# A two-layer graph attention and a transformer block on one core: order of adjacency loads, clips and the first comparison in the opening

## The chip, the cores and the metric

One Trainium2 chip, one of its cores. The metric is the device time of one execution in microseconds (us), the median of several executions. Engines are named as in the profile: PE is the matrix engine (PEld its weight loads), DVE the vector engine, ACT the scalar engine, POOL the general-purpose engine, SP the engine whose queue issues the transfers (SPq in the trace).

## The reference

x has 4096 rows of 256 numbers, and adj is a 4096 x 4096 matrix of 0 and 1 (int32). There are 8 heads of 32 columns.

```python
def gat_layer(x, adj, W, a):
    Wh  = einsum('nd,hdo->hno', x, W)
    src = einsum('hno,ho->hn', Wh, a[:, :O])
    dst = einsum('hno,ho->hn', Wh, a[:, O:])
    e = leaky_relu(src[:, :, None] + dst[:, None, :], 0.2)
    e = where(adj > 0, e, -9e15)
    return einsum('hnm,hmo->hno', softmax(e), Wh)      # heads side by side

h = elu(gat_layer(x, adj, W1, a1)) + x
x = elu(gat_layer(h, adj, W2, a2)) + h
# then one transformer block: layer norm, q k v, masked attention with the same adj,
# projection, residual, layer norm, gelu feed-forward, residual
```

Only the beginning of the first graph layer is touched here.

## The kernel before

**How a graph layer is computed.** The exponential of a leaky ReLU of a sum has one of two forms, according to the sign of src + dst. The kernel therefore needs, for each head and pair of nodes, only a bit that says which form holds (a comparison of a row of terms with one number per partition), masked with the adjacency. The values, scaled for each form, stand on the other side of a matmul. The 4096 result rows are cut into four blocks (nb) of 1024, the 8 heads into four pairs (p), and the 4096 neighbours into eight groups (g) of four tiles of 128. One triple (nb, p, g) of a layer is one group i of the main loop; there are 256 in the two layers.

For group i:

- `compare(i)` makes t8: for each of four tiles k (mt = 4 g + k) and each head j of the pair, a 128 x 1024 comparison of the row s_b with `L.negd`. On ACT it is a Sign (L1122 in the profile), on DVE a tensor_scalar (L1124). Head 0 is mostly DVE's, head 1 ACT's. A fifth step, `mask` (L1137, on DVE), joins t8 with the adjacency mask.
- PE multiplies 128 x 128 pieces of t8 and of the mask with the values vst (L1463).

Other work is put between the matmuls of a group by fractions of the group's length: the comparison of group i + 2, the preparation of values for later tiles, and the adjacency for later groups.

**Adjacency.** One unit (nb, c, k) is 256 rows by 512 columns of adj, 512 KB. `mask_load` brings it into g_adj (three buffers), `mask_clip` (L867, DVE) turns it into 8-bit numbers in adj_8 (five buffers), `turn_out` transposes it on PE (L892) into one of two turn banks, and `turn_in` copies it from there to the mask on ACT (L898). After every second unit SP writes a piece of the mask to memory (mask_d, L901). Outside the opening each clip issues one more load.

**Preparation** of four tiles (`preparation`): the rows of x are transposed (L991) and copied on ACT to g_ft (L1000); the values are multiplied (L1005); ACT and DVE take four kinds of terms from them (L1018 to L1020 on ACT; L1023, L1036 and L1045 on DVE); `split` puts them into vst as a high half (L1051 on ACT) and a low half (L1054 on POOL). At last the terms of head rows go through g_sr (L1065) to memory (s_d, L1068). From there `s_fetch` reads them back as s_b, one row copied to all 128 partitions, for each head of the pair (L1095).

**The opening** is `begin`. In it the order on PE, ACT, DVE and SP is the order of the program (`manual_schedule`); after it this holds for PE, ACT and DVE, while the order on SP is found by the scheduler. SP's small loads for later stages (e_x, e_terms, and the layer norm's n_g and n_be) are put between by the scheduler too. `begin` handles the adjacency for groups 0 and 1 of block 0: units 0 to 7 (the first three in g_adj, four in buffers of the mask, one in a buffer of t8). `turns[0]` holds units 8 to 11, which group 0 transposes. f_0, v_0, part_0, row_0 are the steps of the preparation of the first four tiles, f_1 to row_1 those of the next four; each is a pair of an out step (PE) and an in step (ACT, DVE).

The lines that decide who makes which comparison:

```python
if (j == 1 or mt in more) and not (i == 0 and k == 0):
    nc.scalar.activation(to.bitcast(I8), s, AF.Sign, bias=negd, scale=-1.0)
else:
    nc.vector.tensor_scalar(to, s, negd, -1.0, op0=ALU.is_ge, op1=ALU.mult, saturate=False)
```

So in group 0 DVE makes head 0 of all four tiles and head 1 of the first, ACT the other three.

Of the kernel before, what the change touches and what calls it, by code (L numbers as in the profile page):

```python
# [751 lines left out]
def graph_attention(  # L752
# [38 lines left out]
    G = 4  # L791
# [61 lines left out]
    def mask_load(nb, c, i, r=None):  # L853

        if r is None:
            r = rows_p.tile([P, 2, G * P], I32, name="g_adj", bufs=3)
        at = STARTS[0][nb] * P + i * 2 * P
        nc.sync.dma_start(
            r,
            adj[at : at + 2 * P, c * G * P : (c + 1) * G * P].rearrange("(k r) m -> k r m", r=2),  # L860
        )
        loaded[nb, c, i] = r

    def mask_clip(nb, c, i, load=True):

        v = rows_p.tile([P, G * P, 2], F8, name="adj_8", bufs=5)
        nc.vector.tensor_scalar(  # L867
            v.rearrange("p m r -> p r m"),
            loaded.pop((nb, c, i)),
            1.0,  # L870
            -(2.0**-30),
            op0=ALU.min,
            op1=ALU.max,
            saturate=False,
        )
        clipped[nb, c, i] = v.rearrange("p m r -> p (m r)").bitcast(F16)
        if load:
            load_ahead(1)
# [26 lines left out]
    def mask_turn(nb, c, i):  # L905
        turn_out(nb, c, i)
        turn_in(nb, c, i)
# [17 lines left out]
    def weights_load(l):  # L925

        w, a = weights[l]
        L = Layer()
        L.a_sb = ep.tile([P, H, 2, O], F32, name="e_terms")
        nc.sync.dma_start(  # L930
            L.a_sb.rearrange("p h s o -> p (h s o)"), spread(a, [[0, P], [1, H * 2 * O]])
        )
        L.w_ext = keep.tile([P, DC, D + 2 * H], F32, name="g_w_ext")
        for c in range(DC):
            nc.sync.dma_start(
                L.w_ext[:, c, 0:D].rearrange("p (h o) -> p h o", o=O),
                w[:, c * P : (c + 1) * P, :].rearrange("h p o -> p h o"),
            )
        L.terms = keep.tile([P, 2, NT, H], F32, name=f"g_terms{l}")
        L.negd = L.terms[:, 1]  # L940
        L.r = keep.tile([P, NT, H], F32, name=f"g_r{l}")
        L.tops = keep.tile([P, NT], F32, name=f"g_tops{l}")
        L.ft = {}
        layers.append(L)

    def weights_steps(l):

        L = layers[l]
        values_ = L.w_ext[:, :, 0:D]
        terms = L.w_ext[:, :, D:].rearrange("p c (k h) -> p c k h", k=2)  # L950
        held = {}

        def step_times(k):
            wa = some.tile([P, H, 2, V1], F32, name="g_prod").rearrange("p h i v -> p (h i v)")
            held[k] = wa[:, : DC * D].rearrange("p (c h o) -> p c h o", c=DC, o=O)
            nc.vector.tensor_tensor(
                held[k],
                values_.rearrange("p c (h o) -> p c h o", o=O),
                L.a_sb[:, :, k, :].unsqueeze(1).to_broadcast([P, DC, H, O]),
                op=ALU.mult,  # L960
            )

        def step_sums(k):
            nc.vector.tensor_reduce(terms[:, :, k, :], held.pop(k), AX.X, ALU.add)

        def step_ends():
            nc.vector.tensor_scalar(terms[:, :, 1, :], terms[:, :, 1, :], -1.0, None, op0=ALU.mult)
            nc.vector.tensor_scalar(values_, values_, UP, None, op0=ALU.mult)

        steps = []  # L970
        for k in range(2):
            steps += [lambda k=k: step_times(k), lambda k=k: step_sums(k)]
        return steps + [step_ends]

    def rows_ahead(l, q, width=D):
        if q < NG:
            r = coming_rows[l, q] = rows_p.tile([P, G, D], F32, name="g_rows")
            rows[l].load(r[:, :, :width], G * q, slice(0, width))
# [119 lines left out]
    def apart(i):  # L1098
        l, nb, p, g = groups[i]
        free = (l > 0 and nb + p > 0) or (nb + 1 == len(TILES[l]) and p + 1 < H // 2)  # L1100
        return g == 6 and free and i < len(groups) - NG

    def compare(i):

        l, nb, p, g = groups[i]
        L, s_b = layers[l], s_of[l, nb, p]
        t8 = s8[i] = t_p.tile([P, 2, NW, G, HB], F8, name="t8")
        more = (7, 11, 15, 23, 27, 31)
        if l > 0 or (nb + 1 == len(TILES[l]) and p + 1 < H // 2):
            more = (3, 7, 11, 15, 19, 23, 27)  # L1110
        if apart(i):
            u8[i] = [rows_p.tile([P, NW, G, HB], F8, name="g_adj", bufs=3) for j in range(2)]

        def step(k):
            mt = g * G + k
            for j in range(2):
                to = t8[:, j, :, k, :]
                s = s_b[:, j, :].rearrange("p (w n) -> p w n", n=HB)
                negd = L.negd[:, mt, 2 * p + j : 2 * p + j + 1]

                if (j == 1 or mt in more) and not (i == 0 and k == 0):
                    nc.scalar.activation(to.bitcast(I8), s, AF.Sign, bias=negd, scale=-1.0)  # L1122
                else:
                    nc.vector.tensor_scalar(  # L1124
                        to, s, negd, -1.0, op0=ALU.is_ge, op1=ALU.mult, saturate=False
                    )

        def mask():
            both = t8.rearrange("p j w g n -> p j (w g n)").bitcast(I32)
            m32 = masks[l, nb][g].rearrange("p w g n -> p (w g n)").bitcast(I32)  # L1130
            for j, u in enumerate(u8.get(i, ())):
                nc.vector.scalar_tensor_tensor(
                    u.rearrange("p w g n -> p (w g n)").bitcast(I32),
                    t8[:, j].rearrange("p w g n -> p (w g n)").bitcast(I32),
                    -1, m32, op0=ALU.bitwise_xor, op1=ALU.bitwise_and,
                )
            nc.vector.scalar_tensor_tensor(  # L1137
                both, m32.unsqueeze(1).to_broadcast(list(both.shape)), SIGNS, both,
                op0=ALU.bitwise_or, op1=ALU.bitwise_and,
            )  # L1140

        return [lambda k=k: step(k) for k in range(G)] + [mask]

    def pair_end(l, nb, p, ev):
# [100 lines left out]
    turns = {}  # L1245
# [3 lines left out]
    for nb in range(1, len(TILES[0])):  # L1249
        units = [(nb, c, k) for c in range(NG) for k in range(2 * NW)]  # L1250
# [21 lines left out]
    def load_ahead(n):  # L1272
        for _ in range(min(n, len(coming))):
            mask_load(*coming.pop(0))
# [13 lines left out]
    def begin():  # L1288

        weights_load(0)  # L1290
        rows_ahead(0, 0)
        rows_ahead(0, 1)

        units = own[: 2 * 2 * NW]
        del coming[: len(units)]
        for k, u in enumerate(units):
            place = None
            if 3 <= k < 7:
                place = mask_p.tile([P, 2, G * P], I32, name="mask")
            elif k == 7:  # L1300
                place = t_p.tile([P, 2, G * P], I32, name="t8")
            mask_load(*u, place)

        def clip(k):
            mask_clip(*units[k], load=False)

        def turn(k):
            mask_turn(*units[k])

        def both(use):  # L1310
            use[0]()
            use[1]()

        (f_0, v_0, part_0, row_0), (f_1, v_1, part_1, row_1) = (
            preparation(0, q, spare_bank, True) for q in range(2)
        )
        for use in f_0 + f_1:
            both(use)
        for step in weights_steps(0):
            step()  # L1320
        for use in v_0[:2]:
            both(use)
        for k in range(2):
            clip(k)
            both(v_0[2 + k])
        both(row_0)
        for k in range(4):
            both(v_1[k])
            part_0[k]()
            if k < 2:  # L1330
                clip(2 + k)
            if k > 1:
                part_1[k - 2]()
        both(row_1)
        s_of[0, 0, 0] = s_fetch(0, 0, 0)
        rows_ahead(0, 2)
        for k in range(4):
            turn(k)
            if k < 2:
                part_1[2 + k]()  # L1340
            clip(4 + k)
        load_ahead(3)
        ahead = turns[0]
        for step in compare(0):
            step()
        for k in range(4, len(units)):
            turn(k)
            mask_clip(*ahead[k - 4])
        for step in compare(1):
            step()  # L1350

# [5 lines left out]
    for i, (l, nb, p, g) in enumerate(groups):  # L1357
# [40 lines left out]
        if i + 2 < len(groups):  # L1398
            steps = compare(i + 2)
# [32 lines left out]
        for n in range(tiles):  # L1432
            w, at = n // PER, slice(n % PER * P, (n % PER + 1) * P)
            for m in range(G):
                s_of_m = [t8[:, j, w, m, at] for j in range(2)]
                heads = vst[g][:, m, 2 * p : 2 * p + 2]
# [949 lines left out]
```

## Time and profile before

| | us |
|---|---|
| median of 3 runs | 3108.01 |
| lowest and highest | 3107.69, 3109.81 |
| the profiled execution, its own time | 3108.51 |
| its span in the profile | 3106.7 |
| first matmul of group 0 (L1463) starts | 39.95 |

The span is what the profile shows from the first to the last instruction; the rest of an execution's time lies around it. Times in the trace are counted from the start of the span. A row of the trace's order of time gives the start, the time until the end of the last instruction in it, engine, line, operation, the tiles written and read, the number of instructions, and in brackets how long the engine had been idle before and what ended that. A stretch of the table of windows gives busy times of the engines within it.

### The profile page before, as it was taken

How to read it: one execution, taken by the hardware profiler on the slowest of the kernel's cores; microseconds unless marked ns; L12 is line 12 of the kernel's file. 1: busy time of each engine (PE TensorE's matmuls, PEld its weight loads, DVE VectorE, ACT ScalarE, POOL GpSimd, SP SyncE). 2: the span in 40 equal slices, each digit the busy share in tenths (PEclk: the TensorE clock that was granted, in tenths of full speed). 3: DMA queues.
4: the chain of work that ended last, by engine and by line, in shares of the span. 5: the costliest groups of instructions: out<-in, count | busy, mean ns of one | idle time of the engine just before them, and what ended most of it. 6: DMA issues, size and time to landing. Idle time of an engine off the chain costs nothing.

```text
span 3106.7 us, 139282 instructions
## 1 busy us (share of the span) xinstructions
PE 3057.2 (98%) x64008; PEld 2716.1 (87%) x64008; DVE 2744.0 (88%) x3105; ACT 2702.0 (87%) x3369; POOL 1263.6 (41%) x567
## 2 busy tenths in 40 slices
PE   6999999999999999999999999999999999999999
PEld 5899999999889999999986888888888888887766
DVE  7999999999989999999986999999999999997221
ACT  6899999999999999999975999999999999997232
POOL 3300000000230000000001999999999999997110
PEclk8999999999999999999999999999999999999999
DMA  8666555431221212112126101010101010013210
GB/s 259 218 200 203 169 173 173 148 91 39 88 67 30 91 57 89 38 57 64 47 87 193 32 24 35 21 42 28 31 25 34 22 38 28 28 34 102 75 34 22
DMA packets 214036, 251.15 MB, mean 81 GB/s; under 512 B 89216, under 2 KB 134528, under 8 KB 213440
## 3 DMA queue, kind: packets, MB, share of 16 engines
q1 hardware_dynamic: 213440, 242.15, 25.2%
q8 instruction: 502, 8.22, 1.1%
q14 instruction: 94, 0.77, 0.1%
HBM read 199.63 MB, written 42.47 MB: 78 GB/s over the span
## 4 chain that ended last, share of the span: by engine, by line
PE 51%; ACT 1%; DVE 1%; issue 0%; DVEq 0%; ACTq 0%
PE u_ps L1897 15%; PE u_av L1929 14%; PE u_dn L1929 8%; PE misc L2262 4%; PE misc L2238 4%; PE bank L1463 3%; PE misc L1834 2%; ACT t L1122 1%; PE misc L1853 1%; PE misc L2197 1%; PE misc L1556 0%; DVE t L1137 0%; PE u_ps L2093 0%; DVE t L1124 0%; DVE u_e L1908 0%
## 5 line engine op out<-in xcount | busy, mean ns | idle before, releaser
L1463 PE MATMUL bank<-vst,t 128*128 128x132 f16 x16384 | 1456.6, 220 | 3.6 <-DVE t L1137 3.0
L1463 PE MATMUL bank<-vst,mask 128*128 128x132 f16 (+1 forms) x10516 | 1372.9, 206 | 0.0
L2145 POOL TENSOR_TENSOR u_both<-u_e 128x1024 f32<-128x1024 f32 x446 | 1044.2, 2387 | 768.8 <-DMA u_k<-half_d 768.5
L1122 ACT ACTIVATE t<-s_b,g_terms 128x1024 int8<-128x1024 f32 x1234 | 1318.6, 1149 | 20.1 <-PE bank L1463 15.2
L1463 PEld LDWEIGHTS <-t 128*128 128x128 fp8e4 x16384 | 1186.0, 96 | 15.8 <-DVE t L1137 5.4
L1908 DVE SCALAR_TENSOR_TENSOR u_e<-u_mask,u_ps 128x1024 f32<-128x1024 uint8 x993 | 1128.3, 1214 | 23.6 <-ACT u_ps L1907 23.2
L1907 ACT ACTIVATE u_ps<-u_ps 128x1024 f32<-128x1024 f32 x993 | 995.6, 1009 | 84.1 <-PE u_ps L1897 29.8
L1463 PEld LDWEIGHTS <-mask 128*128 128x128 fp8e4 x10516 | 921.5, 98 | 0.0
L1137 DVE SCALAR_TENSOR_TENSOR t<-mask,t 128x2048 int32<-128x2048 int32 x256 | 588.1, 2297 | 74.6 <-ACT t L1122 66.2
L1897 PE MATMUL u_ps<-u_q,u_k 128*32 128x512 f16 x8192 | 632.7, 380 | 0.7 <-DVE u_e L1908 0.7
L1929 PE MATMUL u_av<-u_e,u_v 128*32 128x128 f32 x16384 | 602.7, 273 | 0.0
L1124 DVE TENSOR_SCALAR t<-s_b,g_terms 128x1024 fp8e4<-128x1024 f32 x814 | 590.8, 759 | 1.9 <-DMA s_b<-s_d 1.9
L1929 PEld LDWEIGHTS u_av<-u_e,u_v 128*32 128x32 f32 x16384 | 483.6, 110 | 119.6 <-ACT u_ps L1907 0.3
L1054 POOL TENSOR_TENSOR vst<-g_adj,vst 128x528 f16<-128x528 f32 x16 | 19.9, 1241 | 725.7 <-ACT g_big L1018 681.6
L1929 PE MATMUL u_dn<-u_both,u_ones 128*32 128x128 f32 x7136 | 278.4, 273 | 0.0
L1929 PEld LDWEIGHTS u_dn<-u_both,u_ones 128*32 128x32 f32 x7136 | 212.4, 110 | 51.4 <-issue 0.8
L1897 PEld LDWEIGHTS <-u_k 128*32 128x32 f16 x8192 | 231.2, 96 | 18.0 <-issue 3.0
L2245 ACT ACTIVATE u_hid<-misc,n_b 128x512 f32<-128x512 f32 x64 | 43.9, 687 | 140.6 <-PE misc L2238 140.6
L2262 PE MATMUL misc<-u_k,u_hid 128*128 128x256 f32 x512 | 111.9, 380 | 0.0
L2262 PEld LDWEIGHTS misc<-u_k,u_hid 128*128 128x128 f32 x512 | 96.9, 190 | 13.2 <-issue 0.5
L2238 PE MATMUL misc<-ln_cols,u_k 128*128 128x512 f32 x224 | 97.3, 593 | 0.0
L867 DVE TENSOR_SCALAR adj<-g_adj 128x1024 fp8e4<-128x1024 int32 x123 | 89.0, 725 | 3.0 <-DMA g_adj<-in_adj_dram 3.0
(195 smaller groups left out, 1927.7 us busy)
## 6 DMA issues: line engine op xcount, KB each, us to landing
g_adj<-in_adj_dram SPq DMA_DIRECT2D x123, 512.0 KB
s_b<-s_d SPq DMA_DIRECT2D x64, 512.0 KB
mask<-mask SPq DMA_DIRECT2D x128, 256.0 KB
u_mask<-mask SPq DMA_DIRECT2D x64, 256.0 KB
mask<-stage SPq DMA_DIRECT2D x48, 256.0 KB
half_d<-u_halves SPq DMA_DIRECT2D x32, 256.0 KB
u_q<-half_d SPq DMA_DIRECT2D x32, 256.0 KB
rows<-e_x SPq DMA_DIRECT2D x31, 256.0 KB
```

The source lines that it names most:

```text
L867: nc.vector.tensor_scalar(v.rearrange("p m r -> p r m"), loaded.pop((nb, c, i)), 1.0, -(2.0**-30), op0=ALU.min, op1=ALU.max, saturate=False,)
L1122: nc.scalar.activation(to.bitcast(I8), s, AF.Sign, bias=negd, scale=-1.0)
L1124: nc.vector.tensor_scalar(to, s, negd, -1.0, op0=ALU.is_ge, op1=ALU.mult, saturate=False)
L1137: nc.vector.scalar_tensor_tensor(both, m32.unsqueeze(1).to_broadcast(list(both.shape)), SIGNS, both, op0=ALU.bitwise_or, op1=ALU.bitwise_and,)
L1463: nc.tensor.matmul(to, left, right, start=k not in opened, stop=last)
L1897: nc.tensor.matmul(ps[r * O : (r + 1) * O, j, :], k_st[c][:, 2 * u + j, at : at + O], q_st[:, h, :], start=True, stop=True,)
L1907: nc.scalar.activation(ps, ps, AF.Exp, scale=SCALE)
L1908: nc.vector.scalar_tensor_tensor(e, mask, 0.0, ps, op0=ALU.not_equal, op1=ALU.mult)
L1929: nc.tensor.matmul(to[j * O : (j + 1) * O, at], lefts[j], es[j // 2][:, j % 2, at], start=first and part == 0, stop=last and part == PARTS ...
L2145: nc.gpsimd.tensor_tensor(both, es_of[i - 1][u], es_of[i][u], op=ALU.add)
L2238: nc.tensor.matmul(ph, w1_sb[:, k, f * P : (f + 1) * P], hn[:, k, :], start=(k == 0), stop=(k == DC - 1),)
L2262: nc.tensor.matmul(po[:, :D], hid[:, f, at : at + P], w2_sb[:, f, :], start=(f == 0), stop=(f == FC - 1),)
```

## The change

In the first comparison (`compare(0)`) the steps are ordered by head: the four tiles of head 0 first, then the four of head 1. Of head 1 two tiles instead of one are made on DVE, the other two on ACT.

In `begin`, the clips of units 4 and 5 and the turn of unit 0 are put between the value steps of the second preparation, and the loads of units 8 to 10 are issued after clip 4 instead of after clip 7. The turns of units 1 to 4 and the clips of units 6 to 9 stand ahead of the comparison of group 0; the turns of units 5 to 7 and the clips of units 10 and 11 stand within and behind it. No operation is added or removed but for the one comparison that goes from ACT to DVE. After `begin` the program is the same.

```diff
-        def step(k):
+        def step(k, heads=(0, 1)):
             mt = g * G + k
-            for j in range(2):
+            for j in heads:
...
-                if (j == 1 or mt in more) and not (i == 0 and k == 0):
+                if (j == 1 or mt in more) and not (i == 0 and k < 2):
...
+        if i == 0:
+            return [lambda k=k, j=j: step(k, (j,)) for j in range(2) for k in range(G)] + [mask]
         return [lambda k=k: step(k) for k in range(G)] + [mask]
...
         both(row_0)
+        ahead = turns[0]
         for k in range(4):
+            if k == 2:
+                clip(4)
+                load_ahead(3)
+            if k == 3:
+                turn(0)
+                clip(5)
             both(v_1[k])
             part_0[k]()
...
         s_of[0, 0, 0] = s_fetch(0, 0, 0)
         rows_ahead(0, 2)
-        for k in range(4):
-            turn(k)
-            if k < 2:
-                part_1[2 + k]()
-            clip(4 + k)
-        load_ahead(3)
-        ahead = turns[0]
-        for step in compare(0):
+        for k in range(2):
+            turn(1 + k)
+            part_1[2 + k]()
+            clip(6 + k)
+        for k in range(2):
+            turn(3 + k)
+            mask_clip(*ahead[k])
+        steps = compare(0)
+        for step in steps[:G]:
             step()
-        for k in range(4, len(units)):
-            turn(k)
-            mask_clip(*ahead[k - 4])
+        turn(5)
+        for step in steps[G : 2 * G]:
+            step()
+        mask_clip(*ahead[2])
+        steps[-1]()
+        turn(6)
+        mask_clip(*ahead[3])
+        turn(7)
         for step in compare(1):
             step()
```

## The prediction

> **What bounds the kernel now.** I read the busy shares first, then a table of stretches, then the order of time on each engine in the opening.
>
> ```profile
> PE 3057.2 (98%) x64008; PEld 2716.1 (87%) x64008; DVE 2744.0 (88%) x3105; ACT 2702.0 (87%) x3369; POOL 1263.6 (41%) x567
> ```
>
> TensorE is busy 98% of the span, so the 2% that it waits is all that a change of order can win. Where that lies is in the table (columns: stretch, its length, PE, PEld, DVE, ACT, POOL busy, granted clock, DMA share, GB/s):
>
> ```profile
> 20.00:30.00 10.00, 3.25 (x27) 2.29 (x26) 7.41 (x17) 6.36 (x20) 9.22 (x8) 0.71 0.48 118
> 30.00:40.00 10.00, 1.84 (x16) 1.29 (x14) 7.60 (x9) 5.56 (x9) 0.64 (x1) 0.50 0.95 305
> 40.00:50.00 10.00, 7.91 (x69) 6.99 (x69) 6.87 (x9) 8.31 (x17) 0.00 (x0) 0.76 0.78 242
> 50.00:60.00 10.00, 8.38 (x89) 7.22 (x90) 9.83 (x21) 6.69 (x16) 4.68 (x3) 0.83 0.93 309
> 80.00:90.00 10.00, 8.87 (x118) 7.63 (x116) 10.00 (x19) 8.04 (x20) 6.15 (x4) 1.00 0.89 260
> 140.00:160.00 20.00, 20.00 (x383) 20.00 (x381) 19.65 (x23) 20.00 (x26) 0.00 (x0) 1.00 0.67 224
> ```
>
> Three stages: up to 50 us all engines have gaps; from 50 to about 120 us DVE is full and sets the pace; from 140 us TensorE is full. In the second stage the mask steps (L1137) start at 60.69, 74.57, 88.50, 102.36 and 116.23, one group of 13.87 us after the other. So a microsecond saved before 50 us on the chain that feeds DVE is handed on to the end, if nothing in between needs a fixed time. That chain, in order of time on DVE, ACT and PE:
>
> ```profile
> 31.11 0.69 DVE L867 TENSOR_SCALAR adj<-t 128x1024 fp8e4<-128x1024 int32 x1
> 34.34 2.74 DVE L1124 TENSOR_SCALAR t<-s_b,g_terms 128x1024 fp8e4<-128x1024 f32 x4 [1.89 <-DMA s_b<-s_d]
> 37.60 2.29 DVE L1137 SCALAR_TENSOR_TENSOR t<-mask,t 128x2048 int32<-128x2048 int32 x1 [0.52 <-ACT t L1122]
> 44.80 0.70 DVE L867 TENSOR_SCALAR adj<-g_adj 128x1024 fp8e4<-128x1024 int32 x1 [3.02 <-DMA g_adj<-in_adj_dram]
> 47.59 2.29 DVE L1137 SCALAR_TENSOR_TENSOR t<-mask,t 128x2048 int32<-128x2048 int32 x1
> 50.40 0.42 DVE L1023 TENSOR_REDUCE g_tops<-turn 128x1 f32<-128x256 f32 x1
> ```
>
> ```profile
> 34.34 3.23 ACT L1122 ACTIVATE t<-s_b,g_terms 128x1024 int8<-128x1024 f32 x3 [4.25 <-DMA s_b<-s_d]
> 39.69 5.29 ACT L1122 ACTIVATE t<-s_b,g_terms 128x1024 int8<-128x1024 f32 x5
> ```
>
> ```profile
> 39.95 0.40 PE L1463 MATMUL bank<-vst,t 128*128 128x132 f16 x2 [0.78 <-DVE t L1137]
> 45.51 0.38 PE L892 MATMUL turn<-g_ident_h,adj 128*128 128x128 f16 x4 [1.34 <-DVE adj L867]
> 51.47 0.53 PE L892 MATMUL turn<-g_ident_h,adj 128*128 128x128 f16 x4 [2.22 <-DVE ev_broad L1036]
> ```
>
> Head 1's row of s_b lands at 34.34 (head 0's by 31.71). Then three signs on ACT, the mask of group 0, four late turns on ACT, five signs of group 1, and the mask of group 1 at 47.59. DVE also sits 3.0 us for an adjacency load issued only at about 40.5, since g_adj has three buffers. The wait of PE at 45.51 is put down to DVE, but DVE's clip there feeds a later turn; the turn bank it needs is freed by ACT's g_ft copy (44.89), queued behind the five signs.
>
> **Adjacency loads further ahead.** Three loads (units 8 to 10) move from SP's 30.53 to behind the first four s_d writes (end 19.23). They wait for clips 0 to 2 (the last ends at 21.36), so they run in 19.3 to 25 us, where the stretches show DMA at 0.48; they pass the second four s_d writes (ready at 23.25). Their bytes leave the crowded 28 to 39 us, and the 3.0 us wait goes: the next load (unit 11) needs only clip 8, so it is issued at about 31 to 33 instead of 40.5. What is late next is ACT, below.
>
> **SP's other order.** As built, four n_ loads (24.86 to 26.79 on SP, some 1,000 tiny packets in 26 to 28 us) leave the place ahead of s_b for later, and e_x and e_terms, before at 19.27 and 19.77 (2.1 us of full DMA in 20 to 23 us), take that place. The second g_sr copy waits for one turn copy more (0.58), so s_d is written 0.6 later. s_b was issued at 26.96 without a wait; now at 26.4 to 27.4, its first bytes at 28.5 against 28.0. I take its second row at 34.85, half a microsecond late. Ends: 33.3, if its slow tail (123 to 184 GB/s in 30 to 32 us) runs at the 300 of the s_b load in 57 to 59 us; 36.5, if everything moved ahead of it stays in its way. The second s_b pair moves from 54.7 and 65.6 to about 48 and 51, the n_ loads into 60 us and later.
>
> **Clips 4 and 5 under POOL.** They move to 22.9 and 26.2 us, where DVE idled 1.81 and 0.78 us. POOL runs its subtractions there without a break:
>
> ```profile
> 22.32 1.67 POOL L1054 TENSOR_TENSOR vst<-ev_broad,vst 128x528 f16<-128x528 f32 x1
> 23.94 1.15 POOL L1054 TENSOR_TENSOR vst<-g_prod,vst 128x528 f16<-128x528 f32 x1
> ```
>
> The first had a clip (22.30, 0.69) beside it and took 0.52 longer; a clip that met POOL at 29.6 took 1.64 instead of 0.69. By the Trainium skill, SBUF — State Buffer, section "Who interferes with whom", DVE in a two-port mode and POOL exclude each other for a whole instruction. The row agrees, and the rule speaks against the change: the gap is not free. Worked out: POOL 22.9 to 24.0, clip 4 to 24.6, POOL to 25.7 (was 25.1), product, POOL to 26.8 and 27.95, clip 5 to 28.6, last products done at 29.75 (was 28.44). Four clips, as before, take 3.36: DVE is free at 33.1, against 31.7 without the rule.
>
> **The comparison by heads.** DVE does head 0 at once (four, 2.74): to 35.85. Two tiles of head 1 follow (0.67 each, one more on DVE than before): 37.2. Clip 10 (0.65): 37.85. Mask 2.29: 40.15, against 39.89. The first step alone gains nothing: TensorE starts 0.25 late.
>
> **ACT.** Turns 0, 4 and 5 move forward into gaps of PE (3.25 of 10 us busy in 20 to 30) and of ACT; the third write of mask_d follows turn 5 on SP, now behind the loads of units 11 and 12, and nobody waits for it in the opening. ACT signs two tiles (2.15) from 34.85, copies two turns instead of four (1.05; the others ran while it sat idle for 4.25), and signs five (5.29): 43.35, against 44.98. Mask 1 then ends at 45.65 (was 49.88), since neither the load nor clips 8 to 10 stand between, and the next clip at 46.25. g_ft's first half is copied by 43.85.
>
> **TensorE to DVE.** From its start to the turn at 45.51 PE worked 4.25 (44.2 less 39.95). So it comes there at 44.45, with the bank free. From that turn to the terms on ACT it took 2.3 (45.51 to 47.81): DVE's first g_tops can start at 46.8, later than DVE's own 46.25. Before: 50.40. **Gain 3.6 us.** The 2.22 wait at 51.47 goes with it (PE arrives when the bank is free). From here the order on DVE, ACT, PE and POOL is that of before.
>
> By the bounds: without the lock 4.1; with s_b at 33.3 and no lock 5.1; with s_b at 36.5, 2.5. I keep the lock and 34.85, each nearest to a row. The profiled run took 3108.51 for a span of 3106.7, 0.50 above the median 3108.01; the span becomes 3103.1 and the median 3104.4.
>
> **The rivals.**
> A larger gain. For: PE ran group 0's start at half clock (0.32 per matmul, later 0.22), so if it is warm its 4.25 shrink by some 1.4. Against: it idles 30.7 to 38.1 as before. With s_b at 33.3 and no lock, 5.1 + 1.4 = 6.5: 3101.5.
> Nothing arrives. DVE, earlier by 3.6, meets adjacency loads that are not, and waits as it did at 44.80. For: DMA share 0.93 in 50 to 60, with s_b moved into it. Against: no such wait after 44.80 in the trace, and a load has 9.5 us from its issue to its clip. 3108.0.
> Slower. The broadcast pair and the tiny n_ loads, now in the DVE-bound stage, make loads land late in every group. It decides from where a load takes over 9.5 us; 2 us late in each of five groups is +10 - 3.6: 3114.4. Against: an s_b row takes 3 us of the queue and only two are moved.
> That s_b itself is late shows a loss only from 34.34 + 4.4 = 38.7 us on, beyond my bound.
>
> **How the numbers follow.** 0.2% is 6.2 us, about what a measurement of this kernel can tell from no change; so my forecast, a gain, counts as no change. Forecast (2.5 to 5.1 gained): 0.68. Larger gain: 0.14, nearly all past 6.2. Nothing arrives: 0.10. Slower: 0.08. Range 3101.0 to 3108.2: forecast, nothing, and the near part of the larger gain. Faster 0.14, same 0.78, slower 0.08.
>
> **What would show it.** Right: g_adj loads on SP in 19 to 25 us; clip 4 stretched to about 1.7 us; s_b's wait on ACT ending near 34.9; five signs directly after two turns, ending near 43.4; no 3.0 wait of DVE for g_adj; mask 1 at 43.4; g_tops near 46.8; mask steps still 13.87 apart. Wrong: s_b past 36.5 or before 33.3, DVE waiting for g_adj after 50 us, or mask steps with another distance.

## The result, and the profile after

| | before | after |
|---|---|---|
| median, us (19 runs each, side by side) | 3108.26 | 3103.35 |
| lowest and highest | 3107.49, 3110.15 | 3102.19, 3105.72 |
| ratio, 95% interval | | 0.9983, 0.9977 to 0.9989 |
| profiled execution: its own time / its span | 3108.51 / 3106.7 | 3105.72 / 3103.8 |

The changed kernel is 4.9 us (0.17%) faster. The forecast was 3104.4 with a gain of 3.6: a real gain, since the interval is 1.9 us to either side, but inside the 0.2% (6.2 us) that the forecast took for about the least that can be told from no change. The profiled execution of after is the longest of its 19, so its trace shows only 2.9 us of the 4.9. A second profile of the same kernel ("after_again" below) took 3102.72, nearer to the median. The two are read together, because the step in which they differ turned out to be the one that decides.

The busy shares of after, and its stretches with the columns as before:

```profile
PE 3054.6 (98%) x64008; PEld 2714.1 (87%) x64008; DVE 2743.6 (88%) x3106; ACT 2701.2 (87%) x3368; POOL 1265.6 (41%) x567
```

```profile
20.00:30.00 10.00, 2.59 (x24) 1.82 (x23) 9.29 (x19) 6.05 (x16) 9.22 (x7) 0.80 0.70 228
30.00:40.00 10.00, 1.32 (x11) 0.82 (x8) 7.50 (x10) 3.85 (x7) 0.65 (x1) 0.50 0.97 301
40.00:50.00 10.00, 8.51 (x76) 7.78 (x77) 8.47 (x11) 8.53 (x17) 0.00 (x0) 0.68 0.83 263
50.00:60.00 10.00, 8.72 (x115) 7.46 (x113) 9.48 (x18) 8.67 (x20) 5.46 (x4) 1.00 0.91 305
80.00:90.00 10.00, 9.02 (x111) 7.80 (x109) 10.00 (x14) 7.74 (x23) 5.46 (x4) 1.00 0.83 250
140.00:160.00 20.00, 20.00 (x380) 20.00 (x378) 19.64 (x23) 20.00 (x24) 0.00 (x0) 1.00 0.68 203
```

The DMA share in 20 to 30 us rose from 0.48 to 0.70: the three adjacency loads are there. In 30 to 40 us the memory traffic is as dense as before, and ACT is busy less. From 80 us on the rows are much the same. The order of time on DVE, ACT, PE and SP in after (one comparison more on DVE; L1478 is before's L1463):

```profile
33.63 2.74 DVE L1124 TENSOR_SCALAR t<-s_b,g_terms 128x1024 fp8e4<-128x1024 f32 x4 [1.83 <-DMA s_b<-s_d]
36.84 1.42 DVE L1124 TENSOR_SCALAR t<-s_b,g_terms 128x1024 fp8e4<-128x1024 f32 x2 [0.47 <-DMA s_b<-s_d]
39.06 2.29 DVE L1137 SCALAR_TENSOR_TENSOR t<-mask,t 128x2048 int32<-128x2048 int32 x1 [0.20 <-ACT t L1122]
45.22 2.29 DVE L1137 SCALAR_TENSOR_TENSOR t<-mask,t 128x2048 int32<-128x2048 int32 x1 [1.27 <-ACT t L1122]
48.38 0.42 DVE L1023 TENSOR_REDUCE g_tops<-turn 128x1 f32<-128x256 f32 x1 [0.26 <-ACT g_terms L1020]
```

```profile
36.84 2.19 ACT L1122 ACTIVATE t<-s_b,g_terms 128x1024 int8<-128x1024 f32 x2 [5.96 <-DMA s_b<-s_d]
39.89 5.30 ACT L1122 ACTIVATE t<-s_b,g_terms 128x1024 int8<-128x1024 f32 x5
```

```profile
41.41 0.40 PE L1478 MATMUL bank<-vst,t 128*128 128x132 f16 x2 [9.89 <-DVE t L1137]
```

```profile
18.39 3.67 SPq L858 DMA_DIRECT2D g_adj<-in_adj_dram  x3
23.52 1.28 SPq L1068 DMA_DIRECT2D s_d<-g_sr  x4
25.54 0.77 SPq L930 DMA_DIRECT2D e_terms<-in_L_gnn_a_dram  x1
28.13 0.81 SPq L1095 DMA_DIRECT2D s_b<-s_d  x2
```

The 3.02 us wait of DVE for an adjacency load is gone, and no adjacency load is waited for after it. What holds DVE now is s_b (1.83 and 0.47) and then ACT's five signs (1.27). And s_b is late here: SP issued it at 28.13, and head 1's row landed at 36.84, 2.0 us after the forecast.

The same rows of after_again:

```profile
31.16 4.21 DVE L1124 TENSOR_SCALAR t<-s_b,g_terms 128x1024 fp8e4<-128x1024 f32 x6
42.33 2.29 DVE L1137 SCALAR_TENSOR_TENSOR t<-mask,t 128x2048 int32<-128x2048 int32 x1 [1.27 <-ACT t L1122]
45.15 0.42 DVE L1023 TENSOR_REDUCE g_tops<-turn 128x1 f32<-128x256 f32 x1
```

```profile
33.95 2.19 ACT L1122 ACTIVATE t<-s_b,g_terms 128x1024 int8<-128x1024 f32 x2 [3.62 <-DMA s_b<-s_d]
37.00 5.30 ACT L1122 ACTIVATE t<-s_b,g_terms 128x1024 int8<-128x1024 f32 x5
```

```profile
26.41 0.82 SPq L1095 DMA_DIRECT2D s_b<-s_d  x2
```

Here DVE makes all six comparisons without a wait for s_b, head 1's row lands at 33.95, and g_tops starts at 45.15. The row landed 2.89 us earlier than in after, g_tops came 3.23 earlier, and the span is 2.9 shorter: between these two profiles what s_b wins or loses goes to the end nearly one for one.

### The profile page after: what moved, and what is told of

Read it like the earlier page. It is cut to its first block, busy times and chain, and to the rows that moved or that the text cites. A ratio compares the mean times of both kernels' runs of the same rounds, so it can differ in the third digit from the quotient of the medians.

```text
span 3103.8 us, 139284 instructions
## 1 busy us (share of the span) xinstructions
PE 3054.6 (98%) x64008; PEld 2714.1 (87%) x64008; DVE 2743.6 (88%) x3106; ACT 2701.2 (87%) x3368; POOL 1265.6 (41%) x567
## 3 DMA queue, kind: packets, MB, share of 16 engines
q8 instruction: 502, 8.22, 1.1%
## 4 chain that ended last, share of the span: by engine, by line
PE 61%; ACT 6%; DVE 4%; issue 1%; DVEq 0%; ACTq 0%
PE u_ps L1912 14%; PE u_av L1944 14%; PE bank L1478 13%; PE u_dn L1944 8%; ACT t L1122 5%; PE misc L2277 4%; PE misc L2253 4%; PE misc L1849 2%; DVE t L1137 1%; DVE u_e L1923 1%; DVE t L1124 1%; PE misc L1868 1%; PE misc L2212 1%; DVE g_adj L1132 0%; ACT ev_broad L1488 0%
## 5 line engine op out<-in xcount | busy, mean ns | idle before, releaser
L1478 PE MATMUL bank<-vst,t 128*128 128x132 f16 x16384 | 1456.5, 220 | 12.7 <-DVE t L1137 12.0
L1478 PE MATMUL bank<-vst,mask 128*128 128x132 f16 (+1 forms) x10516 | 1372.6, 206 | 0.0
L1478 PEld LDWEIGHTS <-t 128*128 128x128 fp8e4 x16384 | 1186.4, 96 | 24.6 <-DVE t L1137 14.4
L1478 PEld LDWEIGHTS <-mask 128*128 128x128 fp8e4 x10516 | 920.8, 98 | 0.0
```

The source lines that it names most:

```text
L1478: nc.tensor.matmul(to, left, right, start=k not in opened, stop=last)
```

## The experiments

In the table L is the landing of head 1's row of s_b, read as the start of ACT's first sign of group 0; mask 0 and mask 1 are the starts of the mask steps of groups 0 and 1; g_tops is the start of DVE's first preparation step after them. Each row is from that kernel's one profiled execution; the last three columns are from all its runs beside the kernel before, whose median was 3108.58, 3108.46 and 3107.97 in the three series.

| kernel | L | mask 0 | mask 1 | g_tops | span | median | ratio | 95% |
|---|---|---|---|---|---|---|---|---|
| before | 34.34 | 37.60 | 47.59 | 50.40 | 3106.7 | 3108.26 | | |
| after | 36.84 | 39.06 | 45.22 | 48.38 | 3103.8 | 3103.35 | 0.9983 | 0.9977–0.9989 |
| after_again | 33.95 | 36.17 | 42.33 | 45.15 | 3100.9 | 3103.41 | 0.9984 | 0.9977–0.9991 |
| loads_only | 34.82 | 38.08 | 47.71 | 50.52 | 3107.4 | 3109.52 | 1.0003 | 0.9994–1.0011 |
| turns_only | 34.91 | 38.16 | 48.30 | 51.12 | 3108.3 | 3110.00 | 1.0002 | 0.9994–1.0010 |
| heads_only | 33.76 | 35.98 | 47.09 | 49.90 | 3106.0 | 3107.83 | 0.9999 | 0.9990–1.0007 |
| clips_late | 35.29 | 37.51 | 47.34 | 50.15 | 3106.6 | 3107.43 | 0.9996 | 0.9987–1.0005 |
| after_no_heads | 33.67 | 36.93 | 43.09 | 46.63 | 3102.4 | 3104.39 | 0.9988 | 0.9979–0.9997 |
| s_b_halves | 38.66 | 41.81 | 47.04 | 50.37 | 3106.3 | 3108.09 | 1.0000 | 0.9991–1.0009 |
| s_b_behind_rows | 35.05 | 38.33 | 43.43 | 47.79 | 3103.4 | 3104.39 | 0.9986 | 0.9977–0.9995 |
| small_later | 33.83 | 36.27 | 42.22 | 45.14 | 3102.3 | 3104.00 | 0.9987 | 0.9977–0.9996 |
| small_and_loads_later | 33.13 | 41.29 | 46.27 | 49.39 | 3105.7 | 3107.82 | 0.9999 | 0.9989–1.0009 |
| sign_to_dve | 33.40 | 35.99 | 41.62 | 44.77 | 3100.4 | 3102.52 | 0.9982 | 0.9973–0.9992 |
| small_later_sign | 34.67 | 36.89 | 42.54 | 45.72 | 3101.4 | 3102.95 | 0.9982 | 0.9973–0.9992 |

Two things before the single runs. Span less g_tops lies between 3055.4 and 3057.2 in all fourteen profiles: the kernels differ by what happens before g_tops, and it is handed on, to within these 1.8 us. And an interval is 2 to 3 us to either side: the medians of the kernels with the gain (3102.5 to 3104.4) stand apart from those without it (3107.4 to 3110.0), but within either set a difference of a microsecond is read from the traces, not from the medians.

**after_again: the changed kernel, a second profile.**

> The changed kernel once more. The theory (the landing of head 1's row of s_b sets the gain, microsecond for microsecond): a profile whose s_b lands earlier than the 36.84 us of the first profile has its first g_tops of group 0's values earlier than 48.38 by as much, and a shorter span than 3103.8. The rival (the gain is made elsewhere, and the first profile differed by chance): the span does not follow s_b. Median by both: 3103.4, ratio 0.9984.

Median 3103.41, as in the result. Its profile is the one shown above: L differs by 2.89 us between two executions of one program. That the two were on one chip is not on record, but the times within each of the two series spread by as much (3102.19 to 3105.72, 3102.17 to 3105.04).

**loads_only, turns_only, heads_only: one part of the change each, put into the kernel before.**

```diff
 loads_only
         for k in range(4):
+            if k == 2:
+                load_ahead(3)
             both(v_1[k])
...
-        load_ahead(3)
 turns_only
         for k in range(4):
+            if k == 2:
+                clip(4)
+            if k == 3:
+                turn(0)
+                clip(5)
             both(v_1[k])
...
-        for k in range(4):
+        for k in range(2):
+            turn(1 + k)
+            part_1[2 + k]()
+            clip(6 + k)
+        for k in range(3, 6):
             turn(k)
-            if k < 2:
-                part_1[2 + k]()
-            clip(4 + k)
         load_ahead(3)
...
-        for k in range(4, len(units)):
-            turn(k)
-            mask_clip(*ahead[k - 4])
+        for k in range(4):
+            if k > 1:
+                turn(4 + k)
+            mask_clip(*ahead[k])
 heads_only
-        def step(k):
+        def step(k, heads=(0, 1)):
...
-            for j in range(2):
+            for j in heads:
...
-                if (j == 1 or mt in more) and not (i == 0 and k == 0):
+                if (j == 1 or mt in more) and not (i == 0 and k < 2):
...
+        if i == 0:
+            return [lambda k=k, j=j: step(k, (j,)) for j in range(2) for k in range(G)] + [mask]
```

> The kernel before with one part of the change: units 8 to 10 are loaded early. The theory: DVE's wait of 3.0 us for an adjacency load goes, but ACT still copies four turns before its five signs, so mask 1 starts at the landing of s_b plus 10.7: with s_b at 34.9 to 36.8, 45.5 to 47.5 against 47.59. Gain 0 to 2 us, 3106.3 to 3108.3. The rival (the early loads are the whole gain): mask 1 near 45, 3103.4.

> The kernel before with one part of the change: clips 4 to 7 and turns 0 to 5 ahead of the first comparison, the loads late and the comparison as before. The theory: ACT has its five signs done near 44.0 instead of 44.98, but DVE still waits for the fourth late load until about 44.8, so mask 1 starts where it did. Gain 0 to 0.5, 3107.7 to 3108.3. The rival (the turns off ACT's path are the gain): 3104 to 3105.

> The kernel before with one part of the change: the first comparison by heads with two tiles of head 1 on DVE. The theory: mask 0 starts about 1.1 us earlier (36.5 for 37.60), and the late load is issued as much earlier, so mask 1 starts near 46.5. Gain about 1, 3107.2. The rival (no part counts without the loads): 3108.3.

None of the three gains anything that can be measured, and their medians less that of before (3108.58) add to +1.6 us, while together they make -4.9. The parts are worth nothing singly; clips 8 to 10 ahead of mask 0, which need the early loads, are in none of the three. Why is seen in DVE's and SP's rows of loads_only:

```profile
44.93 0.70 DVE L867 TENSOR_SCALAR adj<-g_adj 128x1024 fp8e4<-128x1024 int32 x1 [2.75 <-DMA g_adj<-in_adj_dram]
```

```profile
41.01 0.55 SPq L858 DMA_DIRECT2D g_adj<-in_adj_dram  x1
```

The wait did not go away. In before it is the fourth clip behind mask 0, that of unit 11, that waits (3.02 us), and its load was issued at 40.53; here it is the same clip, and its load was issued at 41.01. That load needs a g_adj buffer, a buffer is freed by a clip, and the clip of unit 8 still stands behind mask 0. Having units 8 to 10 early does not help it. In heads_only the mask comes early (35.98), and DVE then waits again:

```profile
39.60 0.70 DVE L867 TENSOR_SCALAR adj<-g_adj 128x1024 fp8e4<-128x1024 int32 x1 [0.65 <-DMA g_adj<-in_adj_dram]
40.92 0.70 DVE L867 TENSOR_SCALAR adj<-g_adj 128x1024 fp8e4<-128x1024 int32 x1 [0.62 <-DMA g_adj<-in_adj_dram]
44.30 0.70 DVE L867 TENSOR_SCALAR adj<-g_adj 128x1024 fp8e4<-128x1024 int32 x1 [2.68 <-PE turn L892]
```

The last is put down to PE, but it is the clip of unit 11, whose load left SP only after clip 8 at 38.25.

**clips_late: everything of the change, but clips 8 to 10 behind mask 0.**

```diff
             turn(3 + k)
-            mask_clip(*ahead[k])
...
-        mask_clip(*ahead[2])
         steps[-1]()
+        for k in range(3):
+            mask_clip(*ahead[k])
         turn(6)
```

> The changed kernel with clips 8 to 10 put back behind mask 0; loads, turns and the order by heads stay as changed. The theory (an early load is worth something only if the clip that frees its buffer is early too): unit 11's load is issued only after clip 8, at about 39 to 41, DVE waits 2 to 3 us for it, and mask 1 starts near 46.5 to 47.5. Gain over before 0 to 1, 3107.5 to 3108.5. The rival (the parts each count a little, and this takes one away): 3104.5.

```profile
44.55 0.70 DVE L867 TENSOR_SCALAR adj<-g_adj 128x1024 fp8e4<-128x1024 int32 x1 [2.94 <-DMA g_adj<-in_adj_dram]
```

Three clips moved back bring the wait back (2.94), and no gain is left that can be told: 0.9996. Together with loads_only this shows that the early loads pay only through the early clips, which free the buffers for unit 11 and the units after it.

**after_no_heads: everything but the comparison by heads and the second tile on DVE.**

```diff
-                if (j == 1 or mt in more) and not (i == 0 and k < 2):
+                if (j == 1 or mt in more) and not (i == 0 and k == 0):
...
-        if i == 0:
-            return [lambda k=k, j=j: step(k, (j,)) for j in range(2) for k in range(G)] + [mask]
...
         steps = compare(0)
+        turn(5)
         for step in steps[:G]:
-            step()
-        turn(5)
-        for step in steps[G : 2 * G]:
             step()
```

> The changed kernel with the first comparison in its old order and with three signs on ACT. The theory: mask 0 starts 3.25 instead of 2.2 after the landing of s_b's second row, and mask 1 9.4 instead of 8.4 after it: 1.0 us less gain, 3104.4. The rival (the order by heads is what lets the early loads count): 3107 to 3108.

From L to mask 1 it takes 9.42 us (43.09 less 33.67), against 8.38 in both profiles of after: ACT has one sign more, about 1.05. The median is 1.0 above after's, as the theory had it, but that is less than the intervals can tell, so the microsecond rests on the trace. ACT is not its only way: mask 0 comes 3.26 after L instead of 2.22, and there ACT's three signs end at 36.90 and DVE, busy with four comparisons and a clip after L, starts the mask at 36.93 without a wait: the two come out together. The order by heads and the tile moved to DVE are not told apart. Nor does any run take the early turns alone out of the changed kernel: their share of the 4.9 us is not shown.

**s_b_halves: s_b read in two halves, the first half as soon as the first s_d writes are out.**

```diff
+        s_b = s_of[0, 0, 0] = s_p.tile([P, 2, W], F32, name="s_b")
...
+        def fetch_half(c):
+            for j in range(2):
+                row = s_d[0][j : j + 1, c * HB : (c + 1) * HB]
+                nc.sync.dma_start(s_b[:, j, c * HB : (c + 1) * HB], spread(row, [[0, P], [1, HB]]))
...
                 clip(4)
+                fetch_half(0)
                 load_ahead(3)
...
-        s_of[0, 0, 0] = s_fetch(0, 0, 0)
+        fetch_half(1)
```

> The changed kernel with the first s_b fetched in two halves of 512 columns: the first straight after the first four writes of s_d, the second where the whole was. Half of its bytes leave the crowded stretch. The theory: s_b is complete 1.5 to 3 us earlier, before DVE is free (31.2 in the second profile of the changed kernel), so mask 0 starts near 36.0 in every run: 3102.5, and less spread than 3102.2 to 3105.7. The rival (s_b does not set the gain): 3103.4 as before.

A miss. The order on SP became another: the four n_ loads stand ahead of the second half, and each is issued only after a long pause, which the trace puts down to the landings of adjacency loads (3.4 us in all) and of s_b's first half (0.8).

```profile
26.80 0.40 SPq L1530 DMA_DIRECT2D n_g<-in_L_gnn_g_dram  x1
28.65 0.40 SPq L1530 DMA_DIRECT2D n_be<-in_L_gnn_be_dram  x1
30.02 0.37 SPq L1530 DMA_DIRECT2D n_g<-in_L_gnn_g_dram  x1
31.40 0.37 SPq L1530 DMA_DIRECT2D n_be<-in_L_gnn_be_dram  x1
32.09 0.82 SPq L1334 DMA_DIRECT2D s_b<-s_d  x2
```

```profile
38.66 2.19 ACT L1122 ACTIVATE t<-s_b,g_terms 128x1024 int8<-128x1024 f32 x2 [7.04 <-DMA s_b<-s_d]
```

It is useful all the same. L is 38.66, g_tops 50.37 and the gain zero: the prediction had put the point from which a late s_b eats everything at 38.7 (its own bound, a gain of 2.5 with s_b at 36.5, would give 39.0).

**s_b_behind_rows: s_b issued behind the g_rows load instead of ahead of it.**

```diff
-        s_of[0, 0, 0] = s_fetch(0, 0, 0)
         rows_ahead(0, 2)
+        s_of[0, 0, 0] = s_fetch(0, 0, 0)
```

> The changed kernel with two loads of rows of x (1 MB together) ahead of the first s_b on the queue instead of behind it. The theory: s_b lands 0.5 to 1.5 us later than in the changed kernel, and everything behind it as much later: 3104 to 3105. The rival (DVE's late free time hides s_b): 3103.4.

SP issued s_b at 26.64, without e_x and e_terms ahead of it, and L is 35.05, 8.41 us after the issue, about a microsecond longer than in most profiles, as the theory had it. Median 3104.39, not to be told from after. Here g_tops comes 12.74 after L, not 11.2 to 11.5: head 0's row was late too, DVE waited for it until 33.75 and made all six comparisons after it, so mask 0 came 3.28 after L instead of 2.22, and TensorE, from 40.67 on, had a granted clock of 0.50 up to 46 us. The landing of head 1's row sets g_tops only where head 0's is early enough.

**small_later, small_and_loads_later: what stands ahead of s_b in the queue.** A memset ties the small loads to their places in the program; in the second kernel the three adjacency loads are issued behind s_b too.

```diff
 small_later
             held["x"] = block("e_x", O)
+            if (l, nb, p) == (0, 0, 0):
+                nc.vector.memset(held["x"], 0.0)
...
         L.a_sb = ep.tile([P, H, 2, O], F32, name="e_terms")
+        if l > 0:
+            nc.vector.memset(L.a_sb, 0.0)
...
         for name, src in self.vectors.items():
+            nc.vector.memset(self.sb[name], 0.0)
 small_and_loads_later, besides
                 clip(4)
-                load_ahead(3)
...
         s_of[0, 0, 0] = s_fetch(0, 0, 0)
+        load_ahead(3)
         rows_ahead(0, 2)
```

> The changed kernel; the small loads for later stages (e_x, e_terms, the four n_ loads) are tied to their places in the program by a memset of their tiles, so that on SP s_b follows directly on the second four s_d writes. My theory (the gain is handed on from the landing of head 1's row of s_b, and that landing is late because of what stands ahead of it in the queue): s_b issued by 26.5 without e_x and e_terms before it, its second row landing at 32 to 33, mask 1 at 40.5 to 41.5, g_tops at 43.5 to 44.5, median 3101.4. Rival (the tail of the broadcast is slow by itself, and the landing varies whatever stands ahead): landing 34 to 37 as before, median 3103.4.

> The same, and the three early adjacency loads are issued behind s_b instead of behind the first four s_d writes. If the second s_d writes are slow because they are queued behind those loads, SP waits for them less than 2 us and s_b is issued at 25.0 to 25.6; then s_b lands before 33, but clip 8 waits for its load to about 32, DVE starts the comparison at about 33.4, mask 0 comes at 38.3 and the median is 3103.0, so early loads are worth 1.6 us against the version with the small loads late alone. Rival (loads at 19 to 25 us need not be that early): 3101.4 or less.

My theory of the queue falls. In small_later s_b was issued at 26.58 and landed at 33.83, no earlier than in after_again (26.41 and 33.95), though e_x and e_terms are no longer in its way. (Its median of 3104.00 is no better than after's either; its span less g_tops is 3057.2, one of the longest. The memsets of e_x and e_terms on DVE, 0.49 us each at 141 and 325 us, don't explain that: small_later_sign has them too, with 3055.7.) In small_and_loads_later DMA was all but idle (share 0.19 in 20 to 30 us), and SP still waited 2.0 us for the landing of s_d before it could issue s_b at 27.05. So neither the small loads nor the adjacency loads explain the wait. What the second kernel does show is the price of late loads:

```profile
34.72 0.70 DVE L867 TENSOR_SCALAR adj<-g_adj 128x1024 fp8e4<-128x1024 int32 x1 [5.18 <-DMA g_adj<-in_adj_dram]
36.10 0.70 DVE L867 TENSOR_SCALAR adj<-g_adj 128x1024 fp8e4<-128x1024 int32 x1 [0.69 <-DMA g_adj<-in_adj_dram]
```

With the earliest s_b of all (33.13) the gain is gone (0.9999): DVE waits 5.18 and 0.69 us for the loads and begins the comparison at 36.71, 3.3 later than I had expected. Early issue of the loads is worth 3.8 us here (3107.82 against 3104.00).

**sign_to_dve, small_later_sign: in group 1 ACT's tile of head 0 goes to DVE.**

```diff
-                if (j == 1 or mt in more) and not (i == 0 and k < 2):
+                if (j == 1 or mt in more) and not (i == 0 and k < 2) and not (i == 1 and j == 0):
```

> The changed kernel; in the second comparison (group 1) the one tile of head 0 that ACT makes is made by DVE, so ACT has four signs there. Theory: mask 1 waits for ACT (1.27 us in the changed kernel's trace), ACT ends 1.06 earlier, DVE has 0.69 more, so mask 1 comes 0.58 earlier, 3102.8. Rival (TensorE's turn or the terms on ACT hold g_tops in any case): 3103.4.

> Small loads late and the sign on DVE together. If both theories hold, 3101.4 - 0.6 = 3100.8; if the landing of s_b does not move, 3102.8; if neither, 3103.4.

Rows of sign_to_dve on DVE:

```profile
41.62 2.29 DVE L1137 SCALAR_TENSOR_TENSOR t<-mask,t 128x2048 int32<-128x2048 int32 x1
44.77 0.42 DVE L1023 TENSOR_REDUCE g_tops<-turn 128x1 f32<-128x256 f32 x1 [0.24 <-ACT g_terms L1020]
```

The wait of mask 1 for ACT is gone, and in its place g_tops waits 0.24 for the terms. From L, mask 1 comes after 8.22 and 7.87 us in the two kernels (8.38 in after), g_tops after 11.37 and 11.05 (11.54 and 11.20 in after): of 0.58 expected some 0.15 reach g_tops. That is mostly the rival: TensorE and the terms on ACT hold g_tops. Its median of 3102.52 is the lowest of all, but 0.9 below after's is less than the intervals can tell. It beats the kernel before; that it beats after is not shown. small_later_sign, with 3102.95, is near the 3102.8 expected if the landing of s_b does not move, and as little to be told from after.

## Why the prediction was right, step by step

**Loads, clips, waits: right.** The three loads run from 18.39 on, the 3.0 us wait went, and the load of unit 11 was issued at 31.30, as forecast (31 to 33). That the gain hangs on the clips as much as on the loads is what loads_only and clips_late showed.

**s_b: the form right, the spread too small.** The prediction had s_b issued at 26.4 to 27.4 and landing at 34.85, with bounds of 33.3 and 36.5. The profile of after is outside both (28.13 and 36.84), so one of the prediction's own signs of being wrong, s_b past 36.5, is there. The four other profiles with that opening, or one sign less on ACT, (after_again, small_later, sign_to_dve, small_later_sign) have 33.40 to 34.67. The value was near, but the bounds came from one execution, and the landing moves by 3 us from one execution to another. For the same reason the times that the prediction named as signs of being right are met in neither profile: g_tops was to start at 46.8 and starts at 48.38 and 45.15. What held is the distances behind s_b.

**The start of the opening: taken from one execution.** TensorE's first 16 products of values (L1005) took 4.92 us in the profile of before, 4.15 in after, and 3.83 in after_again and in heads_only, which has before's program up to there. POOL's first subtraction starts at 19.53, 18.60, 18.05 and 18.27. The prediction worked from the latest of these.

**The rule on DVE and POOL: right in kind, its size 1.0 instead of 1.3, and not on the path.** The prediction took from the Trainium skill, "SBUF — State Buffer", section "Who interferes with whom", that a DVE instruction in a two-port mode and a POOL instruction exclude each other. DVE's and POOL's rows of after:

```profile
22.44 2.24 DVE L867 TENSOR_SCALAR adj<-mask 128x1024 fp8e4<-128x1024 int32 x2
25.62 0.69 DVE L867 TENSOR_SCALAR adj<-mask 128x1024 fp8e4<-128x1024 int32 x1
29.57 2.24 DVE L867 TENSOR_SCALAR adj<-g_adj 128x1024 fp8e4<-128x1024 int32 x2
```

```profile
24.08 1.60 POOL L1054 TENSOR_TENSOR vst<-ev_broad,vst 128x528 f16<-128x528 f32 x1
25.64 2.78 POOL L1054 TENSOR_TENSOR vst<-g_prod,vst 128x528 f16<-128x528 f32 x2
```

Clips 3 and 4 took 2.24, where loads_only's three unhindered ones (at 40.28) take 1.90, and POOL's single subtraction took 1.60, where one without a clip beside it took 1.15 in before. Clip 5 went otherwise than forecast: the prediction let it wait behind two subtractions, to 28.6, but it ran at once (25.62, 0.69), and the two subtractions took 2.78 instead of the 2.25 of loads_only. From POOL's first subtraction to the last product on DVE it is 9.85 us in both profiles of after and 8.86 in loads_only and heads_only, which leave clips 4 and 5 later. So the early clips do cost 1.0. But with the earlier start of the opening DVE is done with its four clips at 31.8 in after and 31.2 in after_again, not at 33.1. In after it then waits 1.83 for s_b; in after_again, where it has no wait there, mask 0 starts 0.19 later than DVE would be ready, because of ACT, and mask 1 waits 1.27 for ACT. So the 0.5 us that the prediction took off for the lock (a gain of 3.6 instead of 4.1) was not lost.

**From s_b to mask 0: the term that was too large.** Because DVE was to be free so late, the prediction started mask 0 at 37.85, 3.0 after L. It starts 2.22 after L in both profiles, when ACT's two signs are done.

**ACT: right.** Five signs directly after two turns, ending 8.35 us after L; the prediction's 43.35 less 34.85 is 8.50. Mask 1 comes 8.38 after L, forecast 8.55.

**TensorE to DVE: right, and a little small in after.** From the start of mask 0 to g_tops, by way of TensorE, the prediction has 8.95 (46.8 less 37.85). It is 8.98 in after_again and 9.32 in after. The difference goes with TensorE's granted clock, which leaves 0.50 about 3.5 us after the first matmul of group 0 in after_again (0.99 in 42 to 43 us) and about 5 us after it in after (0.50 up to 46, 0.77 in 46 to 47). From L to g_tops the sum was 11.95; the profiles say 11.54 and 11.20.

**The sum.** The median of after is 0.6 to 0.7 above after_again's profiled time, so by the one-for-one rule a usual landing is at about 34.6, an estimate. Against the forecast that gives 0.25 for s_b, some 0.6 for the way from L to g_tops, and 0.2 for what follows at once: from g_tops to the next mask step it takes 10.12 (48.38 to 58.50) instead of 10.29, the PE wait of 2.22 having gone with the change, which the prediction named but did not count. 3.6 and these make 4.65 of the 4.9, an estimate; the rest is within what span less g_tops varies. That the usual landing is so near the forecast is luck in part: in single executions it lies up to 2 us off.

**The stage period and the rivals.** After's mask steps start at 58.50, 72.37, 86.29, 100.16 and 114.03: 13.87 to 13.92 apart, as before. DVE waits for no adjacency load from 50 to 135 us, so neither "nothing arrives" nor "slower" took place, though the n_ loads (66.62 and 70.44) and the second s_b pair (51.06 and 52.73) did move into that stage. "A larger gain" by a warm TensorE did not come either: the granted clock in 30 to 40 us is 0.50 in both.

## What to carry to other kernels

A prefetch into a ring of buffers is as early as the instruction that frees the buffer; moving the loads that already have a buffer leaves the wait of the next one where it was. Before a gain is expected from one part of a chain, ask which part is late next: here parts that were worth nothing singly were worth 4.9 us together. And a bound on a transfer's landing that was read in one execution is too narrow; a second profile of the same program shows how far it moves.

## What the runs showed of the hardware that was not expected

**A landing that varies without a cause in the program.** From its issue to head 1's row, s_b took 7.0 to 7.5 us in ten of the profiles that read it whole (7.38 in before, 7.54 in after_again, 7.25 in small_later), but 8.71 in after, 8.41 in s_b_behind_rows and 6.08 in small_and_loads_later. Two of these may have a cause: s_b_behind_rows has 1 MB of rows of x ahead of s_b, and small_and_loads_later has emptier memory traffic ahead of it; each was seen once. For after's 8.71 the program has none. Of the 2.89 us by which the row landed later in after than in after_again, 1.17 lie here, 1.16 between the second s_d writes and the issue of s_b, and 0.56 in the opening before those writes.

**Writes of 4 KB that are slow to land.** Between the last s_d write and the issue of s_b that waits for it lay 1.8 to 2.3 us in most profiles that show the wait (1.83 in after_again, 2.25 in small_and_loads_later) and 3.0 to 3.4 in three (after, loads_only, clips_late). Those three have the early loads ahead of the write, but so have others with 1.8. What makes the longer wait stays open.

**The same matmuls in the opening, 3.8 to 4.9 us.** TensorE's first 16 products of values (128x272, f32) took 3.83 us in three profiles and 4.92 in before, with 4.70 to 4.88 in turns_only, clips_late and s_b_halves, though the program up to there is one and the same and the granted clock is 1.00 in all. What POOL and DVE do next starts later by as much (POOL's first subtraction at 19.53 in before, 18.27 in heads_only). The cause stays open.
